# Second mamba block's input: from TensorE turns to block transfers and VectorE turns

## The chip, the core and the metric

One core of one Trainium2 chip runs the whole program. The metric is device time in microseconds (us), lower is better. The kernel before took 1117.68 us (median of 3 runs, 1117.55 to 1117.88).

## What is computed

The reference is a stack of four layers over 2 sequences of 1024 tokens with 512 features. Each layer adds its output to its input and normalises the sum. Only the first layer, a mamba-2 block, is touched here. Cut to what matters:

```python
zxbcdt = einsum('bld,di->bli', hidden_states, W_in)     # 512 -> 1024 gate | 1024 x | 16 B | 16 C | 16 dt
gate, xBC, dt = split(zxbcdt)
xBC = silu(conv4_causal(xBC) + conv_b)                  # 4 taps along the tokens, by channel
dt  = softplus(dt + dt_bias);  dA = exp(-exp(A_log) * dt)
h_t = h_{t-1} * dA_t + (dt_t * x_t) (x) B_t             # 16 heads of 64 by 16 states
y_t = h_t . C_t + D_skip * x_t
out = rmsnorm(y * silu(gate)) * norm_w @ W_out
x   = layernorm(x + out)
```

The later layers (a ternary projection, a gated recurrence, a dequantised SwiGLU) are the same in both kernels.

## The kernel before

The 2048 tokens are worked on in four blocks of 512 tokens (`TB`), called 0 to 3 here. For the first projection TensorE needs the block's input with features on the partitions: a tile `xT` of 128 partitions by 4 groups (k) by 512 tokens, of which two buffers exist. It comes in two ways.

- **Blocks 0 and 1**: `transposed` (lines 227 to 254) takes the token tiles `X[b]`, which are loaded anyway, and turns them on TensorE: 16 transposes of 128x128 into four PSUM banks (`pt`, line 237), each bank then copied to `xT`. For block 1 ScalarE makes all four copies (line 251, `by_act`).
- **Blocks 2 and 3**: `load_blocks` (line 260) reads the same input again from HBM in four transfers of 256 KB, in pieces of 32 floats (128 bytes), so that 32x32 squares lie where they have to be; `turn_blocks` (line 271) then turns the squares in place on VectorE, four instructions of 128x512.

`head(b, st)` (line 378) makes `xT`, then the small projection `pbc` (line 393: eight matmuls in order of k, two for each k, which give B, C and dt), and what follows from it. For block 1 it stops at its first `yield`, after `pbc` has been copied out, its convolution started and its rows sent by a transfer on SP's queue (line 410).

The opening of block 0 is written out by hand in `opening` (line 624). It runs under a manual schedule for TensorE, VectorE and ScalarE: these three engines run their instructions in the order of the text. It interleaves

- `inner(m)`: the projection `px` of x, eight times (line 372, four matmuls in two passes each), with the first tap of its convolution on ScalarE (line 355); the rest of a convolution is three VectorE taps (line 361) and a silu on ScalarE (line 365). The convolutions wait in the list `later`.
- `scans(h0)`: for four heads a broadcast `pl` on TensorE (line 574) and a scan on VectorE (line 578).
- `weigh(h0)`: `bdec` on VectorE (line 588) and four products on GpSimd (line 593).
- `next(g)`: a gate projection `pg` on TensorE (line 372) and its silu on ScalarE (line 747).
- `next(coming)`: `head(1)` up to its first `yield`.

The end of the opening has this order:

```python
scans(8); weigh(8)
later.append(inner(6)); next(g)
scans(12); weigh(12)
next(coming)                       # block 1: 16 transposes, 4 copies, pbc
later.pop(0)()                     # convolution 4
later.append(inner(7)); later.pop(0)()
for conv in later: next(g); conv() # convolutions 6 and 7
st["dtx"] = by_token(st, 0)        # pxt, line 674
```

`by_token` turns the result of the convolutions on TensorE (`pxt`), and the recurrence (`recur`, line 687) follows, with the rest of the gate projections between its steps. PSUM has eight banks, handed round among all these products.

On SP's queue before the opening stand, one after another, the input tokens of block 0, the weights `w_in`, the tokens `X[1]`, the weights `w_out` and the tokens `X[2]` (lines 84 to 134). `by_blocks(b, st)` (line 802) makes the tile `xT` and issues `load_blocks`; it is called for blocks 2 and 3.

Of the kernel before, what the change touches and what calls it, by code (L numbers as in the profile page):

```python
# [37 lines left out]
def model_kernel(ctx: ExitStack, tc: tile.TileContext, t: dict, out: bass.AP):  # L38
    nc = tc.nc
# [186 lines left out]
    def transposed(pool, b, X, tags=("xT",), split=False, bufs=1, by_act=False, behind=False, soon=False):  # L226


        pieces = [
            pool.tile([P, NK, TB], F32R if split else F32, tag=tag, name=f"{tag}{b}", bufs=bufs)  # L230
            for tag in tags
        ]
        xT = pieces[0]
        for k in range(NK):
            pt = bank("pt")
            for j in range(NJ):
                nc.tensor.transpose(  # L237
                    pt[:, j * P : (j + 1) * P], X[b][:, j, k * P : (k + 1) * P], ident
                )
            if split:  # L240
                copied = nc.scalar.copy(xT[:, k, :], pt)
                if behind:
                    tc.keep_in_program_order(copied)
                nc.vector.tensor_tensor(
                    pieces[1][:, k, :], pt, xT[:, k, :].bitcast(F32), ALU.subtract
                )
            elif soon:
                with tc.high_priority():
                    nc.scalar.copy(xT[:, k, :], pt)
            elif k % 2 or by_act:  # L250
                nc.scalar.copy(xT[:, k, :], pt)
            else:
                nc.vector.tensor_copy(xT[:, k, :], pt)
        return pieces
# [6 lines left out]
    def load_blocks(dst, rows, pinned=False):  # L261

        blocks = rows.rearrange("(n t) (k a c) -> a t k n c", t=32, k=NK, c=32)
        for a in range(4):
            load = nc.sync.dma_start(
                dst[32 * a : 32 * a + 32].rearrange("t k (n c) -> t k n c", c=32), blocks[a]
            )
            if pinned:
                tc.keep_in_program_order(load)

    def turn_blocks(dst, src=None, pinned=False):
        for k in range(NK):
            turned = nc.vector.transpose(dst[:, k, :], (src or dst)[:, k, :])
            if pinned:
                tc.keep_in_program_order(turned)
# [102 lines left out]
    def head(b, st):  # L378

        if b >= 3:  # L380
            X.append(tokens())
            nc.sync.dma_start(X[b], xin[b])
        if b > 1:
            xT = st["xT"]
            turn_blocks(xT, pinned=True)
        else:
            xT = st["xT"] = transposed(mp, b, X, bufs=2, by_act=b > 0)[0]

        pm = bank("pbc")
        half = TB // 2  # L390
        for k in range(NK):
            for i in range(2):
                nc.tensor.matmul(
                    pm[i * 64 : i * 64 + NR, :half], w_bc[:, k, :],
                    xT[:, k, i * half : (i + 1) * half], start=(k == 0), stop=(k == NK - 1),
                )
        rows = mp.tile([P, 3 + TB], F32, tag="xpad", name="rpad", bufs=3)
        for i in range(2):
            nc.scalar.copy(
                rows[:NR, 3 + i * half : 3 + (i + 1) * half], pm[i * 64 : i * 64 + NR, :half]  # L400
            )
        BC = st["BC"] = mp.tile([NBC, TB], F32, tag="BC", name="BC")

        mix = started(rows[:, 3:], NBC, b, NX, cwr, cbr, BC, rows)
        tk = sp.tile([P, 2, NJ, NH], F32, tag="tk", name="tk")
        dt, bt = st["dt"], st["bt"] = tk[:, 0], tk[:, 1]
        if b:

            turn = mp.tile([P, P], F32, tag="a2", name="turn")
            nc.sync.dma_start(  # L410
                turn[:HJ], rows[32:NR, 3:].rearrange("h (j t) -> h j t", t=P)
            )
        if b < 2:
            yield
        if b:

            mix(b == 1)
            nc.sync.dma_start(turn[HJ:], BC[:NS].rearrange("n (j t) -> n j t", t=P))
            nc.sync.dma_start(crow[b], BC[NS:])
            st["CT"] = mp.tile([P, TB], F32, tag="rows", name="CT", bufs=2)  # L420
            nc.sync.dma_start(st["CT"], crow[b].unsqueeze(0).to_broadcast([8, NS, TB]))
            yield
            yield from by_rows(b, turn, tk)
            return

        z = sp.tile([P, NJ, NH], F32, tag="z", name="z", bufs=1)
        a = sp.tile([P, NJ, NH], F32, tag="a", name="a", bufs=1)
        pdt = bank("pdt")
        for j in range(NJ):
            nc.tensor.transpose(  # L430
                pdt[:, j * NH : (j + 1) * NH], rows[32:NR, 3 + j * P : 3 + (j + 1) * P],
                ident[32:NR, 32:NR],
            )
        nc.vector.tensor_tensor(
            z, pdt[:, : NJ * NH].rearrange("p (j h) -> p j h", h=NH),
            dtb.unsqueeze(1).to_broadcast([P, NJ, NH]), ALU.add,
        )
        softplus(dt.rearrange("p j h -> p (j h)"), z.rearrange("p j h -> p (j h)"), NJ * NH)
        nc.vector.tensor_tensor(a, dt, rootA.unsqueeze(1).to_broadcast([P, NJ, NH]), ALU.mult)
        nc.vector.scalar_tensor_tensor(  # L440
            a, a, 1.0e18, rootN.unsqueeze(1).to_broadcast([P, NJ, NH]), ALU.min, ALU.mult
        )
        nc.vector.tensor_tensor(a, a, endless.unsqueeze(1).to_broadcast([P, NJ, NH]), ALU.min)
        for lo in (0, 32):
            nc.vector.tensor_scalar(a2[:, :, lo : lo + NH], a, LOG_FLOOR, None, ALU.max)
        yield
        pa = bank("pa")
        for j in range(NJ):
            nc.tensor.transpose(pa[:NR, j * P : (j + 1) * P], a2[:, j, :], ident)
        dA, cum = tmp("dA")[:NR], tmp("cum")[:NR]  # L450
        nc.scalar.activation(dA, pa[:NR, :], AF.Exp)

        r = st["r"] = mp.tile([NR, TB], F32R, tag="rows", name="rows", bufs=2)
        nc.scalar.activation(r, pa[:NR, :], AF.Exp)
        yield
        nc.vector.tensor_tensor(r[32:NR], dA[32:NR], r[32:NR].bitcast(F32), ALU.subtract)
        nc.vector.memset(r.bitcast(F32).rearrange("r (j t) -> r j t", t=P)[:, :, 0:1], 0.0)
        mix()
        yield
        for j in range(NJ):  # L460
            w = slice(j * P, (j + 1) * P)
            nc.vector.tensor_tensor_scan(
                cum[:, w], dA[:, w], zeros[:NR].to_broadcast([NR, P]), 1.0, ALU.mult, ALU.add
            )
        rc = st["rc"] = mp.tile([NR, TB], F32R, tag="rows", name="rows", bufs=2)
        nc.scalar.copy(rc, cum)
        yield
        nc.vector.tensor_tensor(rc[32:NR], cum[32:NR], rc[32:NR].bitcast(F32), ALU.subtract)
        yield
# [151 lines left out]
        st["dtx"] = by_token(st, 0)  # L621
        yield

    def opening(st, own, g, coming):


        inner, crows, grams, spans, scans, weigh = parts(0, st)
        first = inner(0)
        later = [inner(1)]
        next(own)  # L630
        first()
        next(own)
        later.append(inner(2))
        scans(0)
        later.append(inner(3))
        next(own)
        crows()
        later.pop(0)()
        next(own)
        later.append(inner(4))  # L640
        grams()
        spans()
        later.append(inner(5))
        weigh(0)
        later.pop(0)()
        scans(4)
        weigh(4)
        next(g)
        later.pop(0)()
        scans(8)  # L650
        weigh(8)
        later.append(inner(6))
        next(g)
        scans(12)
        weigh(12)
        next(coming)
        later.pop(0)()
        later.append(inner(7))
        later.pop(0)()
        for conv in later:  # L660
            next(g)
            conv()
        st["dtx"] = by_token(st, 0)
# [138 lines left out]
    def by_blocks(b, st):  # L802

        st["xT"] = mp.tile([P, NK, TB], F32, tag="xT", name=f"xT{b}", bufs=2)
        load_blocks(st["xT"], xin_rows[b])

    H, before, st = None, None, {}
    own, coming = head(0, st), {}
# [1 line left out]
    with tc.manual_schedule(  # L810
        engines={mybir.EngineType.PE, mybir.EngineType.DVE, mybir.EngineType.Activation}
    ):
        next(own)
        exponents(alog, endless, rootA, rootN)
        next(own)
        cwx, cbx, normw, dskip = columns_of_layer()
        opening(st, own, g, ahead)
    for b in range(NBLK):
        if b:
            g, coming = gates(b, st), {}  # L820
# [624 lines left out]
```

## Time and profile before

| | us |
|---|---|
| median of 3 runs | 1117.68 |
| the profiled execution | 1116.89 |
| its span, first to last instruction | 1115.1 |
| TensorE busy (PE) | 1099.4 |
| VectorE busy (DVE) | 701.4 |
| ScalarE busy (ACT) | 451.4 |
| GpSimd busy (POOL) | 366.8 |

The profile is of one execution, which took 0.79 us less than the median. Times in it count from the start of the span. In the timeline a row gives the start, the time from the first start to the last end of the merged instructions, the engine, the line, what is written from what, and in brackets the idle time before it with what ended it. PE is the matmul row of TensorE, PEld its weight loads. A float32 matmul is two passes, and so two rows ("x16" are eight matmuls).

### The profile page before, as it was taken

To read this page: it belongs to the slowest core of one execution; us is meant where nothing else is said; L and a number is where in the kernel's file an instruction comes from. 1 tells how busy PE (TensorE), PEld (TensorE's weight loads), DVE (VectorE), ACT (ScalarE), POOL (GpSimd) and SP (SyncE) were. 2 spreads that over 40 slices of the span, in tenths; PEclk is the share of its full clock that TensorE was granted. 3 is DMA by queue.
4 is the path that set the end of the run, shared out by engine and by line. 5 is a ranking of instruction groups with operands and counts; after the bars stand their busy time and mean duration, and the time that the engine had idled before them with its cause. 6 is when DMAs were issued, how large, how long until landed. Compare 5 with 4: busy or idle time off the path is not lost.

```text
span 1115.1 us, 12073 instructions
## 1 busy us (share of the span) xinstructions
PE 1099.4 (99%) x4450; PEld 663.3 (59%) x4450; DVE 701.4 (63%) x1267; ACT 451.4 (40%) x690; POOL 366.8 (33%) x347
## 2 busy tenths in 40 slices
PE   8999999999999999999999999999999999999996
PEld 5455445445544555745444444447888888888885
DVE  5989797797869676875727437184238866325224
ACT  3334624463454233556653372553223224224223
POOL 1547471565348240254433231236511001001000
PEclk9999999999999999999999999999999999999999
DMA  8005200911210137245650001304544002100001
GB/s 323 21 9 126 91 1 17 253 30 39 105 81 0 39 135 215 57 94 123 113 113 37 1 1 49 27 0 143 189 94 76 1 1 63 14 1 30 8 1 41
DMA packets 122059, 77.04 MB, mean 69 GB/s; under 512 B 94512, under 2 KB 95312, under 8 KB 120456
## 3 DMA queue, kind: packets, MB, share of 16 engines
q1 hardware_dynamic: 120792, 75.77, 25.7%
q8 instruction: 37, 0.61, 0.2%
q10 hardware_dynamic: 976, 0.39, 0.1%
q14 instruction: 30, 0.25, 0.1%
q0 software_dynamic: 224, 0.02, 0.0%
HBM read 59.95 MB, written 16.02 MB: 68 GB/s over the span
## 4 chain that ended last, share of the span: by engine, by line
PE 80%; DVE 11%; ACT 4%; issue 2%; POOL 2%; DMA 1%; SPq 0%; DVEq 0%; ACTq 0%; POOLq 0%
PE pgu L1039 20%; PE p L1069 16%; PE po L1270 10%; PE pg L372 9%; PE px L372 7%; PE po L770 6%; DVE acc L298 3%; PE po L1159 2%; PE py L705 2%; DVE L L578 2%; PE po L987 2%; PE pxt L674 1%; PE pt L237 1%; POOL x L1165 1%; PE py L697 1%
## 5 line engine op out<-in xcount | busy, mean ns | idle before, releaser
L1050 DVE SCALAR_TENSOR_TENSOR h<-pgu,L_ffn_up_scale,sg 128x512 f32<-128x512 f32 x63 | 47.1, 748 | 126.4 <-PE pgu L1039 122.6
L372 PE MATMUL px<-xT,w_in 128*128 128x512 f32 x256 | 114.6, 597 | 0.0
L593 POOL TENSOR_TENSOR L<-L,gm 128x512 f32<-128x512 f32 x64 | 93.5, 1490 | 63.7 <-DVE bdec L588 34.7
L372 PE MATMUL pg<-xT,w_in 128*128 128x512 f32 x256 | 113.5, 594 | 0.0
L770 PE MATMUL po<-w_out,xc 128*128 128x512 f32 x256 | 112.5, 593 | 0.7 <-DVE L L578 0.7
L1069 PE MATMUL p<-cv,w 128*128 128x512 f32 x256 | 110.8, 592 | 0.0
L1039 PE MATMUL pgu<-wF__4239,wg 128*128 128x512 f32 x256 | 101.7, 397 | 0.0
L1039 PE MATMUL pgu<-lo__4240,wg 128*128 128x512 f32 x256 | 100.8, 394 | 0.0
L1039 PE MATMUL pgu<-lo__4240,wu 128*128 128x512 f32 x256 | 100.7, 393 | 0.0
L1039 PE MATMUL pgu<-wF__4239,wu 128*128 128x512 f32 x256 | 100.7, 393 | 0.0
L1270 PE MATMUL po<-wd,hh 128*128 128x512 f32 x252 | 98.3, 396 | 0.3 <-POOL wg L930 0.3
L1270 PE MATMUL po<-wd,hl 128*128 128x512 f32 x252 | 98.3, 396 | 0.2 <-DVE hl L1054 0.2
L1049 ACT ACTIVATE sg<-pgu,L_ffn_gate_scale 128x512 f32<-128x512 f32 x63 | 43.4, 689 | 127.6 <-PE pgu L1039 127.6
L770 PEld LDWEIGHTS po<-w_out,xc 128*128 128x128 f32 x256 | 48.4, 190 | 61.8 <-issue 56.7
L1053 ACT CAST hh<-h 128x512 fp32r<-128x512 f32 x63 | 39.1, 621 | 112.5 <-DVE h L1050 112.3
L1069 PEld LDWEIGHTS p<-cv,w 128*128 128x128 f32 x256 | 48.6, 190 | 60.4 <-issue 58.8
L1069 PE MATMUL p<-xT,w 128*128 128x512 f32 x192 | 82.9, 592 | 0.0
L372 PEld LDWEIGHTS px<-xT,w_in 128*128 128x128 f32 x256 | 47.5, 190 | 57.5 <-issue 55.5
L298 DVE SCALAR_TENSOR_TENSOR acc<-xpad,cols,acc 128x512 f32<-128x512 f32 x72 | 68.5, 953 | 20.0 <-ACT acc L342 15.2
L372 PEld LDWEIGHTS pg<-xT,w_in 128*128 128x128 f32 x256 | 47.3, 190 | 54.2 <-issue 53.1
L1386 POOL TENSOR_TENSOR x<-x,r 128x512 f32<-128x512 f32 x12 | 15.2, 1295 | 195.0 <-DVE r L1385 195.0
L578 DVE TENSOR_TENSOR_SCAN L<-pl,id 128x512 f32<-128x512 f32 x64 | 75.0, 1205 | 4.7 <-ACT pl L572 3.7
(292 smaller groups left out, 1921.9 us busy)
## 6 DMA issues: line engine op xcount, KB each, us to landing
L<-decays SPq DMA_DIRECT2D x12, 1024.0 KB, 8.0
x_mid<-x SPq DMA_DIRECT2D x4, 1024.0 KB, 4.3
x<-x_mid SPq DMA_DIRECT2D x4, 1024.0 KB, 7.5
st<-in_L_ffn_gate_w_dram SPq DMA_DIRECT2D x8, 512.0 KB, 6.4
st<-in_L_ffn_up_w_dram SPq DMA_DIRECT2D x8, 512.0 KB, 4.4
st<-in_L_ffn_down_w_dram SPq DMA_DIRECT2D x8, 512.0 KB, 3.8
x_rec<-x SPq DMA_DIRECT2D x4, 1024.0 KB, 4.3
x<-_attn_hidden_states_dram SPq DMA_DIRECT2D x3, 1024.0 KB, 16.8
```

What stands on the lines that cost most here:

```text
L298: tap = nc.vector.scalar_tensor_tensor(acc, xpad[:, k : k + TB], w[:, k : k + 1], acc, ALU.mult, ALU.add)
L372: nc.tensor.matmul(pm[:n, :], w_in[:, k, lo : lo + n], xT[:, k, :], start=(k == 0), stop=(k == NK - 1),)
L578: nc.vector.tensor_tensor_scan(L[:, h, :], pl, id4.rearrange("p j t -> p (j t)"), 0.0, ALU.mult, ALU.add)
L593: nc.gpsimd.tensor_tensor(L[:, h, :], L[:, h, :], st["gm"], ALU.mult)
L705: nc.tensor.matmul(pys[i][hh * HD : (hh + 1) * HD, q, :], dtx[q][:, 2 * i + hh, :], L[:, h, s], start=(first and q == 0), stop=(q == 1), s ...
L770: nc.tensor.matmul(po, xc[:, m, j * P : (j + 1) * P], w_out[:, m, :], start=(m == 0), stop=(m == NX - 1),)
L1039: nc.tensor.matmul(pm, w[g][:, k, cols], x[:, k, :], start=(k == 0 and x is pieces[0]), stop=(k == NK - 1 and x is pieces[-1]),)
L1049: nc.scalar.activation(sg, pgu[0], AF.Silu, scale=gs[:, m : m + 1])
L1050: nc.vector.scalar_tensor_tensor(h, pgu[1], us[:, m : m + 1], sg, ALU.mult, ALU.mult)
L1053: nc.scalar.copy(halves[0], h)
L1069: nc.tensor.matmul(pm, w1[i][:, k, m * P : (m + 1) * P], rhs[:, k, :], start=(k == 0), stop=(k == NK - 1),)
L1270: nc.tensor.matmul(po[j], x[:, j * P : (j + 1) * P], wd[m // GK][:, m % GK, :], start=(m == 0 and x is h[0]), stop=(m == NF - 1 and x is h ...
```

## The change

Block 1 no longer uses `transposed`. Its `xT` is allocated and its four transfers are issued by `by_blocks(1)` just before the opening, kept in program order on SP's queue. Four VectorE turns, one for each k, are written into the opening: one after `scans(4)`, one after `scans(8)`, two after `scans(12)`, each ahead of the `weigh` that follows. `head(1)` starts with `pbc`. The tokens `X[1]` are loaded as before.

```diff
@@ head @@
-        if b > 1:
+        if b:
             xT = st["xT"]
-            turn_blocks(xT, pinned=True)
+            if b > 1:
+                turn_blocks(xT, pinned=True)
         else:
-            xT = st["xT"] = transposed(mp, b, X, bufs=2, by_act=b > 0)[0]
+            xT = st["xT"] = transposed(mp, b, X, bufs=2)[0]
@@ opening @@
-    def opening(st, own, g, coming):
+    def opening(st, own, g, coming, second):
...
         scans(4)
+        nc.vector.transpose(second[:, 0, :], second[:, 0, :])
         weigh(4)
         next(g)
         later.pop(0)()
         scans(8)
+        nc.vector.transpose(second[:, 1, :], second[:, 1, :])
         weigh(8)
         later.append(inner(6))
         next(g)
         scans(12)
+        nc.vector.transpose(second[:, 2, :], second[:, 2, :])
+        nc.vector.transpose(second[:, 3, :], second[:, 3, :])
         weigh(12)
         next(coming)
@@ by_blocks and its calls @@
-        load_blocks(st["xT"], xin_rows[b])
+        load_blocks(st["xT"], xin_rows[b], pinned=b == 1)
...
-        opening(st, own, g, ahead)
+        by_blocks(1, coming)
+        opening(st, own, g, ahead, coming["xT"])
```

## The prediction

> **What bounds the kernel now.** I read the busy table and the chain of the page first, then the timeline of each engine from 36 to 100 us, where everything that the change touches lies, and last the transfers.
>
> ```profile
> PE 1099.4 (99%) x4450; PEld 663.3 (59%) x4450; DVE 701.4 (63%) x1267; ACT 451.4 (40%) x690; POOL 366.8 (33%) x347
> ...
> PE 80%; DVE 11%; ACT 4%; issue 2%; POOL 2%; DMA 1%; SPq 0%; DVEq 0%; ACTq 0%; POOLq 0%
> ```
>
> TensorE is busy for 99% of the span and is 80% of the chain that ended last. So a microsecond of TensorE work removed is worth a microsecond, provided that TensorE then finds something to do; and a wait put before TensorE costs its whole length. TensorE around the transposes of block 1 (`pt`):
>
> ```profile
> 51.56 1.19 PE L574 MATMUL pl<-rows,pick 48*128 48x512 f32 x4
> 52.68 1.34 PE L237 MATMUL pt<-ident,x 128*128 128x128 f32 x8
> 54.48 1.09 PE L237 MATMUL pt<-ident,x 128*128 128x128 f32 x8 [0.46 <-DVE L L578]
> 55.59 1.93 PE L393 MATMUL pbc<-xT,w_bc 128*48 128x256 f32 x16
> 57.46 3.70 PE L372 MATMUL px<-xT,w_in 128*128 128x512 f32 x8
> 61.00 7.03 PE L372 MATMUL pg<-xT,w_in 128*128 128x512 f32 x16
> ```
>
> There is one small idle in them, 0.46 us inside the transposes themselves. VectorE in the same stretch:
>
> ```profile
> 39.15 4.56 DVE L578 TENSOR_TENSOR_SCAN L<-pl,id 128x512 f32<-128x512 f32 x4 [0.23 <-PE pl L574]
> 43.75 0.42 DVE L588 TENSOR_TENSOR bdec<-L,tk 128x256 f32<-128x256 f32 x1
> 44.09 2.31 DVE L361 SCALAR_TENSOR_TENSOR acc<-px,cols,acc 128x509 f32<-128x509 f32 x3
> 46.32 4.55 DVE L578 TENSOR_TENSOR_SCAN L<-pl,id 128x512 f32<-128x512 f32 x4
> 50.91 0.42 DVE L588 TENSOR_TENSOR bdec<-L,tk 128x256 f32<-128x256 f32 x1
> 52.09 4.57 DVE L578 TENSOR_TENSOR_SCAN L<-pl,id 128x512 f32<-128x512 f32 x4 [0.76 <-PE pl L574]
> 56.69 0.42 DVE L588 TENSOR_TENSOR bdec<-L,tk 128x256 f32<-128x256 f32 x1
> 57.03 8.98 DVE L361 SCALAR_TENSOR_TENSOR acc<-px,cols,acc 128x509 f32<-128x509 f32 x12
> ```
>
> VectorE is nearly full too: it idles for 0.76 us before the last scans and then not until 66.01. So both engines are loaded here, and the change takes work from one and gives it to the other, at a place where the first must wait for the second. That is the question to be worked out.
>
> **What goes.** The 16 transposes (two rows of x8) and the idle between them: from 52.68 to 55.59, **2.91 us of TensorE**. Four copies on ScalarE go as well (2.34 us in all between 53.38 and 56.24); ScalarE has gaps of over a microsecond on both sides of them, so I count them at nothing. Nobody else waits for either.
>
> **What comes on SP's queue.** Four transfers, behind `X[2]`, whose issue ends at 18.34, and ahead of the line 410 transfer, whose issue comes at 58.35 when ScalarE has made its rows; nothing stands between. The load at the start uses every DMA engine until about 29.5:
>
> ```profile
> 18.00:29.00 11.00, 11.00 (x30) 4.63 (x28) 9.96 (x15) 5.72 (x10) 0.00 (x0) 1.00 1.04 387
> 31.00:43.00 12.00, 12.00 (x39) 5.75 (x37) 10.20 (x17) 3.83 (x9) 4.96 (x4) 1.00 0.00 1
> 106.00:112.00 6.00, 6.00 (x21) 2.97 (x20) 4.51 (x4) 2.00 (x5) 5.76 (x5) 1.00 1.41 155
> ```
>
> The last two columns of these stretches are the DMA share and GB/s. The third stretch is the same kind of load for block 2, in pieces of 128 bytes: 155 GB/s. Block 1's 1.05 MB would take 6.8 us at that rate; if none of it moves before 29.5, it has landed at about 36.3, in a stretch in which the DMA engines do nothing today. The first turn wants it at 43.6. That is 7 us in hand, so I cost the transfers at nothing: the empty DMA engines hide them. Without that cover every microsecond of lateness would hold VectorE at the first turn, with the convolutions and scans queued behind it, and so TensorE. `w_out` and `X[2]`, which could be slowed, are not read before 90.
>
> **What comes on VectorE.** Four turns. The trace has the same instruction for block 2:
>
> ```profile
> 166.36 2.48 DVE L273 STREAM_TRANSPOSE xT<-xT 128x512 f32<-128x512 f32 x4
> ```
>
> One takes 0.67 us (664 to 705 ns over block 2 and 3), so they follow each other by (2.48 - 0.67) / 3 = 0.60 us. The scans take 1.205 us each by the page and follow each other by (4.57 - 1.205) / 3 = 1.12. `bdec` must wait for the last scan to be written, so today it starts 4.60 after the first scan; a turn needs nothing from the scans and can start 4.49 after it. With these steps, VectorE runs so:
>
> - Turn 0 starts at 39.15 + 4.49 = 43.64, `bdec` at 44.24 instead of 43.75: 0.49 late. Convolution 3 and scans 8 to 11 follow, from 46.81.
> - Turn 1 at 51.30, `bdec` at 51.90 (0.99 late), after which VectorE is free at 52.24. Today it stood idle until 52.09, waiting for `pl`; that idle pays for most of the first two turns. Scans 12 to 15 begin at 52.24, only **0.15 late**.
> - Turn 2 at 56.73, ending at 57.40; turn 3 at 57.33, ending at **58.00**. The last `bdec` starts at 57.93, 1.24 late.
>
> **What TensorE now waits for.** With the transposes gone it comes to `pbc` at 52.68. The two instruction lists, set side by side, differ on TensorE only in the 16 transposes and in what the matmuls from `pbc` on wait for: the second, third and fourth k of `pbc` wait for VectorE, each for its turn. The bank that `pbc` takes is free when the second gate's silu has read it, at 52.27. The first two k take half of 1.93, to 53.64. The third k can start when turn 2 is written, and TensorE follows VectorE by 0.04 us (the second scan ended at 54.44, `pt` went on at 54.48): 57.44. **TensorE stands for 3.80 us.** The third k takes 0.48, the fourth starts at 58.04 after another 0.12, and `px` of m = 7 starts at 58.52. Today it starts at 57.46. So the sum is 3.80 + 0.12 of waiting, 2.91 saved, and 0.05 for the two hand-overs: **1.06 us late**. The order of the text is what costs: the last two turns stand behind scans 12 to 15, and TensorE has nothing between `pl` and `pbc` but the transposes that are taken out.
>
> **What is late next.** TensorE runs `px` and two `pg` without a gap, then `pxt`, whose last part waits for ScalarE's last silu, and that stands behind the last gate's silu:
>
> ```profile
> 68.06 0.60 ACT L747 ACTIVATE g<-pg 128x512 f32<-128x512 f32 x1 [2.31 <-PE pg L372]
> 68.56 0.62 ACT L365 ACTIVATE xc<-acc 128x512 f32<-128x512 f32 x1
> ```
>
> Convolution 7 ends at 66.01 today, 2.55 before this silu begins. It will end 1.24 later and the silu 1.06 later, so 2.37 remain and VectorE does not set this end. GpSimd's last products end at 62.17 today and are 1.24 later; they are read from 69.49 on. After that the lists of all engines are alike, and every start depends on TensorE's or VectorE's earlier work, not on a clock time; TensorE has only 0.95 us of waiting for VectorE between 70 and 100 (92.79 and 94.00), and that chain begins with `pxt` and moves with it. I take none of it as absorbed; were all of it absorbed, 0.1 would be left.
>
> Bounds: with turns of 0.71 us following by 0.65, as the slowest rows have it, and with 0.1 for each hand-over, the four turns give about 0.3 more, 1.4 in all. The least is 0.1 by absorption. I take 1.1, nearest to the rows. The profiled execution took 1116.89, which becomes 1118.0; it stood 0.79 under the median of the runs, so for the median 1117.68 + 1.1 = **1118.8**.
>
> **A stand of 3.8 us and the clock.** No row of this kernel has TensorE wait for longer than 1.4 us before its last matmul, so the trace does not show what such a stand does to its clock. It shows one longer stand, at the end (last columns: granted clock, DMA share, GB/s):
>
> ```profile
> 1106.50:1111.00 4.50, 0.00 (x0) 0.00 (x0) 3.33 (x10) 1.61 (x5) 1.54 (x2) 1.00 0.49 179
> 1111.20:1115.00 3.80, 0.00 (x0) 0.00 (x0) 0.00 (x0) 0.00 (x0) 0.00 (x0) 0.50 0.23 82
> ```
>
> The last matmul ends at 1106.46; the clock was still full 4.5 us later and half after that. By this row a stand of 3.8 is just short enough. The Trainium skill, "TensorE: Matmul & The Clock Gate", section "The HAM clock gate", speaks against the change: the array falls to half its clock after one idle window of about 3.4 us, and the windows run freely. By that rule an estimate is that a stand of 3.8 holds a whole window in (3.8 - 3.4) / 3.4, some 12%, of executions, and then about 3.4 us of work at half the clock would cost 1.7 us more; the trace's own end, 4.5 us or more, does not contradict it.
>
> **Rivals.**
>
> *The clock falls in the stand (slower).* Place: `px` of m = 7, just after `pbc`. Price: at least what the start of the trace shows, where the first 24 rows of 128x128 (`early`, from 1.43) took 4.73 us and 24 at the pace of the transposes (1.09 for 8) would take 3.27, so 1.46 more; at most all of `px` at half speed, 3.54 more. It decides if it falls in most executions. For it: the stand is near the one after which the clock fell. Against: full at 4.5 us. The sum is 1.06 + 1.46 to 3.54: 1120.2 to 1122.3, say 1121.2.
>
> *The transfers are late (slower).* They would have to land after 44.8 to move the time past 1120; for it: small pieces at 155 GB/s, behind 2 MB of `w_out`. Against: 7 us in hand. Say 1120.5.
>
> *The 2.91 us are kept (faster).* If `pbc` did not stand there waiting, because the turns were done before TensorE came to it, `px` would start at 54.55. Turn 3 would have to end by 54.1, before the scans it stands behind. Against: the order of the list, which has both turns behind those scans, and no other TensorE work between. 1117.68 - 2.91 = 1114.8.
>
> *Absorbed.* The 0.95 us of waiting swallow most: 1117.8.
>
> **How the numbers follow.** The forecast, 1118.4 to 1119.4, gets 0.68; absorbed 0.09; the clock 0.13; late transfers 0.05; kept 0.05. A measurement of this kernel can tell about 0.2%, 2.2 us, from no change. The forecast and the absorbed case lie within it, with a little of the late transfers: 0.78. Above it lie the clock and the rest: 0.17. Below, 0.05. The range goes from the absorbed case, 1117.8, to the lower part of the clock's, 1120.8, and leaves out about 0.05 below and 0.1 above.
>
> **What the profile will show.** Right: no `pt` rows after 10 us; `pbc` in two parts with 3.5 to 4.2 us of idle between, ended by VectorE's turn; scans 12 at 52.1 to 52.5; `px` 7 at 58.4 to 59; `pxt` at 68.9 to 69.4; turns of 0.67; the block load landed by 38. Wrong: `px` 7 before 57.4 (something fills the gap), passes of `px` 7 over 0.8 us (the clock), a turn 0 that waits for a DMA, or a later wait of TensorE that has shrunk by the same microsecond.

## The result and the profile after

The changed kernel took **1120.36 us** (median of 8 runs, 1119.49 to 1121.06), the kernel before 1117.04 beside it (8 runs, 1116.85 to 1117.88): a ratio of 1.0028, 95% interval 1.0018 to 1.0039. It is 3.3 us slower. The forecast of the likeliest case was 1.1 slower; the time lies in the part of the range that belonged to the rival "the clock falls in the stand" (1120.2 to 1122.3). The profiled execution took 1120.36, its span is 1118.6.

| us | forecast | measured |
|---|---|---|
| block 1's transfers landed | 36.3 | between 37 and 38 |
| turn 0 starts | 43.64 | 43.70 |
| scans 12 to 15 start | 52.24 | 52.22 |
| `pbc` third k starts, after a stand of TensorE of | 57.44, 3.80 | 57.43, 3.61 |
| the last `bdec` starts | 57.93 | 57.90 |
| `px` of m = 7 starts | 58.52 | 59.31 |
| `pg` after it starts (before 61.00; forecast 1.06 later) | 62.06 | 64.38 |

First the busy line of the page, which says little: TensorE has 16 matmuls less (4434 rows for 4450) and yet the same busy time, and its share has gone down.

```profile
PE 1099.2 (98%) x4434; PEld 661.9 (59%) x4434; DVE 703.4 (63%) x1271; ACT 449.0 (40%) x686; POOL 366.7 (33%) x347
```

VectorE's timeline in the changed kernel (start, time, engine, line, what is written from what):

```profile
52.22 4.55 DVE L579 TENSOR_TENSOR_SCAN L<-pl,id 128x512 f32<-128x512 f32 x4
56.70 0.68 DVE L658 STREAM_TRANSPOSE xT<-xT 128x512 f32<-128x512 f32 x1
57.30 0.67 DVE L659 STREAM_TRANSPOSE xT<-xT 128x512 f32<-128x512 f32 x1
57.90 0.38 DVE L589 TENSOR_TENSOR bdec<-L,tk 128x256 f32<-128x256 f32 x1
```

Each of these starts within 0.03 of its forecast: the turns take 0.67 to 0.68, follow each other by 0.60, and stand behind the scans. TensorE's timeline:

```profile
52.75 1.07 PE L394 MATMUL pbc<-xT,w_bc 128*48 128x256 f32 x8
57.43 1.95 PE L394 MATMUL pbc<-xT,w_bc 128*48 128x256 f32 x8 [3.61 <-DVE xT L658]
59.31 5.23 PE L372 MATMUL px<-xT,w_in 128*128 128x512 f32 x8
64.38 7.03 PE L372 MATMUL pg<-xT,w_in 128*128 128x512 f32 x16
```

The stand is where it was forecast, for the reason forecast (the bracket names the turn of the third k, line 658). But the two halves of `pbc` are the same eight rows, and the second takes 1.95 for 1.07; `px`, which took 3.70 before, takes 5.23. The stretches of the trace tell why (columns: the busy time of PE, PEld, DVE, ACT and POOL with their instructions, then granted clock, DMA share, GB/s):

```profile
52.20:55.60 3.40, 1.62 (x11) 0.61 (x9) 3.40 (x5) 0.13 (x1) 3.22 (x3) 1.00 0.00 0
55.60:59.00 3.40, 1.57 (x8) 0.61 (x8) 3.36 (x7) 0.00 (x0) 2.36 (x3) 0.50 0.00 0
59.00:62.40 3.40, 3.40 (x6) 1.52 (x5) 3.29 (x5) 2.07 (x4) 3.40 (x4) 0.50 0.05 10
62.40:66.00 3.60, 3.60 (x9) 1.52 (x8) 3.04 (x5) 1.36 (x3) 1.04 (x2) 1.00 0.02 5
```

The granted clock is half from 55.60 to 62.42. It fell 1.78 after TensorE's last row had ended (53.82), in the middle of the stand. From `pg` on the shift against the kernel before stays 3.38 (`pxt` at 71.24 for 67.86), and the span is 3.5 longer: nothing is absorbed later. The mean clock was 0.995 or 0.996 in all 8 runs, and 0.998 in the profile of before, so this is no accident of one execution (a window of 6.83 us at half clock takes 0.003 off the mean).

### The profile page after: what moved, and what is told of

The parts are those of the page before. It is cut to its first block, busy times and chain, and to the rows that moved or that the text cites. A ratio compares the mean times of both kernels' runs of the same rounds, so it can differ in the third digit from the quotient of the medians.

```text
span 1118.6 us, 12047 instructions
## 1 busy us (share of the span) xinstructions
PE 1099.2 (98%) x4434; PEld 661.9 (59%) x4434; DVE 703.4 (63%) x1271; ACT 449.0 (40%) x686; POOL 366.7 (33%) x347
## 4 chain that ended last, share of the span: by engine, by line
PE 81%; DVE 11%; ACT 4%; issue 1%; POOL 1%; DMA 1%; SPq 0%; DVEq 0%; ACTq 0%; POOLq 0%
PE pgu L1045 20%; PE p L1075 18%; PE po L1276 10%; PE pg L372 8%; PE px L372 6%; PE po L775 6%; DVE L L579 3%; DVE acc L298 3%; PE po L993 3%; PE po L1165 2%; PE py L710 2%; PE pxt L679 1%; PE pt L237 1%; POOL x L1171 1%; PE py L702 1%
```

## The experiments

My theory: of the 3.3 us, 1.1 is the stand itself, as forecast, and 2.2 the clock that falls in it. The rivals: the clock is a bystander, and the rest beyond 1.1 comes from what the turns and transfers do elsewhere, on VectorE with all that queues behind the turns, or later in the kernel. The first two kernels shorten the stand of TensorE without moving any turn; the other four move the turns or TensorE's work, to see whether the 2.91 us can be had at all. The first four ran on one chip with a kernel before of 1117.12 (33 runs, 1116.95 to 1117.33), the last two on another with 1117.33 (21 runs, 1116.79 to 1117.90). Each experiment has 11 runs.

### 1. TensorE kept busy in the stand (1118.21 us)

In `head`, inside the loop over k of `pbc`; nobody reads the bank:

```diff
+            if b == 1 and k == 2:
+                fill = bank("fill")
+                for _ in range(13):
+                    nc.tensor.matmul(fill[:, :P], ident, ident, start=True, stop=True)
```

> The changed kernel, with 13 matmuls of the identity by itself put between the second and the third k of block 1's pbc, so that TensorE works through the 3.6 us for which it stood; they write a bank that nobody reads. Theory A (the stand costs 1.06 net, and the rest of the 3.3 us is the clock at half behind it): pbc and px of m = 7 at full pace again (0.97 and 3.7 us), granted clock 1.00 throughout 52 to 66, time about 1.1 over the kernel before, 1118.1. Rival B (the slow passes come from reading what VectorE has just written, or from PSUM, not from the stand): px stays at 5.2 us, time stays 3.3 over, 1120.4. Rival C (filling makes no difference because VectorE sets the end): 1120.4 as well, with px at 3.7 and pxt late by a convolution.

Measured: 1118.21 (1118.05 to 1118.45), 1.0010 of before (1.0001 to 1.0019). TensorE's timeline, and one stretch with the clock in the third column from the right:

```profile
53.67 3.17 PE L396 MATMUL fill<-ident 128*128 128x128 f32 x26
57.36 1.23 PE L398 MATMUL pbc<-xT,w_bc 128*48 128x256 f32 x8 [0.52 <-DVE xT L662]
58.52 3.70 PE L372 MATMUL px<-xT,w_in 128*128 128x512 f32 x8
```

```profile
52.00:66.00 14.00, 13.48 (x64) 7.42 (x63) 13.75 (x19) 4.11 (x9) 10.06 (x9) 1.00 0.02 4
```

`pbc` goes on at the same time as without the filling (57.36 for 57.43), the clock stays full, `px` takes 3.70 again, and it starts at 58.52: to the hundredth what the prediction had. More work on TensorE makes the kernel faster. Against the kernel before of the same chip the filled kernel is 1.09 slower, and the changed kernel 3.32 slower: 1.1 is the turns' lateness, **2.2 the clock**. The filling leaves every turn, transfer and queue of the changed kernel where it was, so whatever theory puts the 2.2 on one of those falls.

### 2. Half of the filling (1119.57 us)

The same with `range(6)`.

> As the run with 13, but with 6 matmuls: TensorE works until about 55.2 and stands for 2.1 us only. Theory A, if a stand must be about as long as the 3.6 us to bring the clock down: clock 1.00, 1118.1. Theory A, if part of a window of idle is enough (the clock fell 1.8 us after the stand began in the changed kernel): the clock falls in some executions, times spread from 1118.1 to 1120.4. Rival B: 1120.4.

Measured: 1119.57 (1118.08 to 1120.47), 1.0017 (1.0008 to 1.0026). The median hides two groups: four executions at 1118.08 to 1118.11, with a mean clock of 0.997 or 0.998, and seven at 1118.71 to 1120.47, six of them with 0.996 (the one at 1118.71 has 0.998). The profile is of one of the seven:

```profile
57.45 1.23 PE L398 MATMUL pbc<-xT,w_bc 128*48 128x256 f32 x8 [2.08 <-DVE xT L662]
58.61 5.40 PE L372 MATMUL px<-xT,w_in 128*128 128x512 f32 x8
```

```profile
55.30:58.60 3.30, 1.22 (x9) 0.34 (x8) 3.30 (x6) 0.00 (x0) 2.27 (x3) 1.00 0.00 0
58.70:62.00 3.30, 3.30 (x4) 1.39 (x5) 3.16 (x6) 2.18 (x4) 3.30 (x3) 0.50 0.08 15
```

A stand of 2.08 is enough to bring the clock down, in about half of the executions, and it falls *after* the stand: `pbc` runs at full clock (1.23) and `px` not. The four that are spared take the time of the first experiment. So the length of a stand does not settle alone what it costs.

### 3. The turns earlier, TensorE's order kept (1117.52 us)

```diff
         scans(4)
         nc.vector.transpose(second[:, 0, :], second[:, 0, :])
+        nc.vector.transpose(second[:, 1, :], second[:, 1, :])
...
         scans(8)
-        nc.vector.transpose(second[:, 1, :], second[:, 1, :])
+        nc.vector.transpose(second[:, 2, :], second[:, 2, :])
+        nc.vector.transpose(second[:, 3, :], second[:, 3, :])
...
         scans(12)
-        nc.vector.transpose(second[:, 2, :], second[:, 2, :])
-        nc.vector.transpose(second[:, 3, :], second[:, 3, :])
```

> The changed kernel with its turns moved up: two after scans 4 to 7, two after scans 8 to 11, none after scans 12 to 15. By the working of the prediction (the place of the last two turns makes the stand): no stand before pbc, px of m = 7 at about 54.7, VectorE's last convolution ends 1.4 us later than before, at 67.4, and its silu frees pxt at 68.0 instead of 69.2: time 1.2 under the kernel before, 1115.8, clock full. Rival (VectorE had no room, any turn on it costs its length): 1.0 or more over before, 1118 to 1119.

Measured: 1117.52 (1116.20 to 1117.76), 1.0000 (0.9991 to 1.0009). Again two groups: five executions at 1116.20 to 1116.32 (mean clock 0.997), six at 1117.52 to 1117.76 (0.996). TensorE in one of the five:

```profile
54.67 3.70 PE L372 MATMUL px<-xT,w_in 128*128 128x512 f32 x8
...
66.18 0.33 PE L679 MATMUL pxt<-ident,xc 128*128 128x128 f32 x1 [0.29 <-ACT xc L365]
68.47 0.33 PE L679 MATMUL pxt<-ident,xc 128*128 128x128 f32 x1 [1.96 <-ACT xc L365]
```

`px` starts at 54.67 for 57.46: nearly all of the 2.91 us has arrived there. But the last parts of `pxt` now wait 0.29 and 1.96 for the silus, and those for VectorE's convolutions, which the four turns and a `bdec` of 0.79 instead of 0.42 push from 57.03 to 58.71. After this wait 0.77 is left (`py` at 68.72 for 69.49), and that is what the five executions gain (0.9 under the kernel before). The expected 1115.8 was missed by 0.4 there. The other six lose 1.39 more, with a lower mean clock; that a stand of about 2 brings the clock down in some executions only is what experiment 2 showed, but no profile here is of one of the six.

### 4. `px` of m = 7 moved before `pbc`, whole (1116.90 us)

```diff
         weigh(12)
+        later.append(inner(7))
         next(coming)
         later.pop(0)()
-        later.append(inner(7))
         later.pop(0)()
```

> The changed kernel with the projection px of m = 7 moved ahead of block 1's pbc, the turns left where the change put them: TensorE has 3.6 us of real work in the stand. Theory A: px from 52.7 to 56.3, pbc from 56.3 with under 0.5 us of waiting, clock full, pxt freed by the last silu at about 68.0: 1.2 under the kernel before, 1115.8. Rival B (slow passes from something other than the stand): px or pbc slow, over 1117. Rival (the gain cannot be had since VectorE is the bound): 1117 to 1118.5.

Measured: 1116.90 (1116.76 to 1117.10), 0.9998 (0.9989 to 1.0007): the expected gain of 1.3 is missing. It is there at 68 (`py` at 68.04 for 69.49) and is lost at 95. The rows of ScalarE and VectorE there:

```profile
93.39 1.28 ACT L489 ACT_TABLE_LOAD   x1 [8.57 <-DVE work L488]
...
95.02 0.42 DVE L490 TENSOR_TENSOR_SCAN work<-work,zeros 64x128 f32<-64x128 f32 x1 [1.72 <-ACT work L489]
```

and one row of the kernel before:

```profile
95.14 0.48 DVE L489 TENSOR_TENSOR_SCAN work<-work,zeros 64x128 f32<-64x128 f32 x1 [0.38 <-ACT work L488]
```

Before, ScalarE loads the table for its next exp at 86.29, while it has nothing to do. Here the load waits for VectorE's `work` at 93.39, and the 1.28 it takes stands on the path. I had moved `inner(7)` with its ScalarE tap, which changes ScalarE's order and the order in which the small rotating buffers are handed out. My reading is that the exp then has to wait for two engines, and that one of the two waits is put on the load; that this is the reason is argued and not shown, and the next kernel, which leaves ScalarE's order alone, speaks for it. On TensorE the loss appears at 126.34, where it waits for VectorE's scans, which follow from the row at 95.02:

```profile
126.34 7.13 PE L775 MATMUL po<-w_out,xc 128*128 128x512 f32 x16 [1.52 <-DVE L L579]
```

The kernel before waits 0.24 there and goes on at 126.52: of the 1.45 gained at 68, 0.18 is left.

### 5. Only the matmuls of `px` moved (1115.65 us)

```diff
-        def inner(m):
-            px = in_proj(xT, DI + m * P, P, "px")
+        def inner(m, px=None):
+            px = px or in_proj(xT, DI + m * P, P, "px")
...
+        px7 = in_proj(st["xT"], DI + 7 * P, P, "px")
         next(coming)
         later.pop(0)()
-        later.append(inner(7))
+        later.append(inner(7, px7))
```

> As the run with px of m = 7 ahead of pbc, but only its matmuls go ahead; its first tap on ScalarE stays behind pbc's copies, so that the rotating buffers of the small tiles are handed out in the order of the changed kernel. In the run before, the recurrence began 1.45 us earlier than in the kernel before, and 1.28 of that was lost at 95 us, where VectorE waited 1.72 us (0.38 in the kernel before) for ScalarE, whose table load for the exponential stood behind VectorE's result at 93.39 instead of being done at 86.29. Theory A (the gain was lost in that table load alone): the load is done in ScalarE's idle time again, and the whole 1.45 stays: 1115.7. Rival (VectorE's own chain of work takes the gain back): 1116.9 again.

Measured: **1115.65** (1115.47 to 1116.39), 0.9986 (0.9977 to 0.9995), faster than both kernels. TensorE:

```profile
52.63 3.70 PE L372 MATMUL px<-xT,w_in 128*128 128x512 f32 x8
56.26 2.29 PE L394 MATMUL pbc<-xT,w_bc 128*48 128x256 f32 x16
...
67.85 0.33 PE L680 MATMUL pxt<-ident,xc 128*128 128x128 f32 x1 [1.47 <-ACT xc L365]
```

The turns are as late as in the changed kernel. The 3.70 of `px`, which needs none of them, now fill the stand; `pbc` loses 0.36 (2.29 for 1.93) and nothing more. The table load is early again (84.90), the scan's wait 0.38. `pxt` stands for 1.47, and the mean clock is 0.997 or 0.998 in all 11 runs. `py` starts at 68.11, 1.38 earlier than before.

### 6. The turns sooner still, and the transfers first (1115.29 us)

Block 1's four transfers are issued ahead of `X[1]`, `w_out` and `X[2]`; two turns go into the 1.13 us in which VectorE stands idle near 33, two after scans 8 to 11:

```diff
+    second_xT = load_second()          # before the load of X[1]
...
         next(own)
+        nc.vector.transpose(second[:, 0, :], second[:, 0, :])
+        nc.vector.transpose(second[:, 1, :], second[:, 1, :])
         later.append(inner(4))
...
         scans(8)
+        nc.vector.transpose(second[:, 2, :], second[:, 2, :])
+        nc.vector.transpose(second[:, 3, :], second[:, 3, :])
```

> The changed kernel with block 1's four transfers put ahead of those of X[1], w_out and X[2] on SP's queue, two turns put where VectorE stood idle for 1.13 us at 33.3, and two after scans 8 to 11, where it stood for 0.76. By the prediction's working (only turns beyond VectorE's idle time cost): VectorE's last convolution ends about 0.4 later than in the kernel before, at 66.4, TensorE has no stand before pbc, pxt is freed at about 67.2 and py starts near 67.4 instead of 69.5: 2.1 under the kernel before, 1115.0, if TensorE's stand before pxt (1.2 us) leaves the clock alone. If the transfers are not in by 33.3, or slow those of w_in down: over 1116. If a turn costs its length wherever it stands: 1116 or more.

Measured: **1115.29** (1115.04 to 1115.84), 0.9983 (0.9974 to 0.9992), the best of all. VectorE has two of its turns at 33.39 and 34.02; TensorE:

```profile
54.59 3.70 PE L382 MATMUL px<-xT,w_in 128*128 128x512 f32 x8
...
67.42 0.33 PE L689 MATMUL pxt<-ident,xc 128*128 128x128 f32 x1 [1.50 <-ACT xc L375]
```

The convolutions start at 57.66, 0.63 late instead of the 1.68 of experiment 3, so the stand before `pxt` is 1.50 instead of 1.96, and the clock stays up in all 11 runs (0.997 to 0.999). `py` starts at 67.68, 1.81 earlier than before. In the profiled execution 0.60 of that is given back at 125.30, where TensorE waits 0.84 for block 1's scans (0.24 before). They are late because two small VectorE instructions at 92.06 and 92.91 took 0.81 and 0.63 instead of 0.33 and 0.52. The profiled execution of experiment 2 shows the same (0.82 and 0.63, then a wait of 0.83), the other profiles do not, so this does not come from the place of the turns; why it happens stays open.

The times of this chip lie in two groups some 0.5 to 0.6 apart, here (1115.04 to 1115.29 and 1115.68 to 1115.84) as in the kernel before (1116.79 to 1117.05 and 1117.33 to 1117.90). Lower group against lower group the gain is 1.9, which fits the 1.81 of `py`, and that of experiment 5 is 1.4, which fits its 1.38; the medians give 2.0 and 1.7.

## Why the prediction was right and wrong

- *"2.91 us of TensorE"* go: right. In experiment 3, where nothing stands before `pbc`, `px` starts 2.79 earlier.
- *Transfers at nothing*: right. They landed 1 to 1.7 later than I had it, and still some 6 before the first turn; no turn waits for a DMA.
- *Four turns of 0.67 by steps of 0.60, scans 0.15 late, the last two turns behind scans 12 to 15*: right within 0.06 in the three rows of the table that show them.
- *"TensorE stands for 3.80 us"*: 3.61, since the first half of `pbc` drains until 53.82, not 53.64. Where it goes on, and so what it costs, was right: 57.43.
- *"1.06 us late"*: right as the price of the order. The filled kernel has `px` at 58.52 as forecast and takes 1.09 more.
- *Absorbed*: nothing was. The shift is 3.38 at 64 and at 71, and still 3.36 at 130.
- **The step that failed: "By this row a stand of 3.8 is just short enough."** I read the end of the trace, where the clock was still full 4.5 us after the last matmul, as the length of stand that the clock bears. It bears less than half of that: it fell 1.78 after TensorE's last row in the profiled execution, and by the mean clock it fell in all 8. What that row really showed was where a window ends. The recorded changes of the clock lie on a grid: in the changed kernel full from 4.40, half from 55.60, 15 steps of 3.413; in experiment 2 7.48 and 58.68, 15 steps; in the kernel before 5.20 and 1111.12, 324 steps. At the end of the trace before, the window that closed at 1107.7 held 1.25 of idle time and left the clock up; the next one closed at 1111.12. The 4.5 was a phase, and no limit.
- *The rule of the Trainium skill* ("TensorE: Matmul & The Clock Gate", "The HAM clock gate": half clock after one idle window of about 3.4 us), which I took to mean a window idle from end to end: the step of the grid agrees, the need for a whole idle window does not. In the changed kernel the window from 52.18 to 55.60 had TensorE at work until 53.82, and the clock fell at its end. The measurement decides; the estimate of 12% of executions made from the rule was far too low, since it was 8 of 8.
- *The price, 1.46 to 3.54*: right. 2.2 by the medians, and 2.32 by `pg` (64.38 for 62.06).
- *The chance of 0.13* was therefore the error, not the mechanism: the forecast's own terms gave 1.1, and the rival was added to it. The forecast, 1118.4 to 1119.4, was missed by 1.0; that the measured 1120.36 lies inside the range (up to 1120.8) is luck, since the range only took in the lower part of a rival held unlikely.
- *The signs*: `pbc` in two parts with 3.61 between, scans 12 at 52.22, turns of 0.67 to 0.69 and the load before 38 came as listed. `px` came at 59.31, after the 58.4 to 59 listed, `pxt` at 71.24 and not at 68.9 to 69.4, and with passes of `px` of up to 1.22 the sign of the clock was there.
- *Kept, 1114.8*: its condition (turns done before TensorE comes to `pbc`) was met in experiments 3 and 6, and the full 2.91 was not kept even so. I had worked out that convolution 7 has 2.37 in hand against the last gate's silu, and did not use it there: a TensorE that runs 2.8 earlier and a VectorE that runs 0.6 to 1.7 later use it up, and `pxt` stands for 1.5 to 2.

## What to carry to other kernels

Price a new stand of TensorE twice, once for its length and once for the clock that falls in it, and take the second as likely from about 2 us on (half of the executions here at 1.96 and 2.08, all at 3.61, none at 1.5), even where the first is nearly paid for by work removed. When work is handed from the bound engine to another, ask what the bound engine does until it comes back: putting a product that needs none of it into the gap (experiment 5), or the handed work into the other engine's idle time well before (experiment 6), turned 3.3 us lost into 1.7 and 2.0 gained by the medians. Move the matmuls alone, and leave the other engines' order as it is: the same move with a ScalarE instruction in tow gained 0.2 instead of 1.7 (experiments 4 and 5).

## What the hardware showed that was not expected

How often the clock fell, by the longest stand of TensorE in the profiled execution behind 50 us and the mean clock of the runs (one window of 3.41 us at half clock takes 0.0015 off the mean; 0.996 and less counts as down):

| stand, us | kernel | clock down |
|---|---|---|
| 3.61 | changed | 8 of 8 |
| 2.08 | experiment 2 | 6 of 11 |
| 1.96, with 0.29 just before | experiment 3 | 6 of 11 |
| 1.40 to 1.52 | experiments 4, 5, 6 | 0 of 33 |

One reading fits all four rows: the clock falls at the end of a window of 3.41 us that holds more than some 1.6 to 1.8 us of idle time, wherever the windows happen to lie, and rises at the end of a busy one. The windows of the profiled executions, laid out from the recorded changes of the clock, bound it:

| window | kernel | idle time in it, us | clock at its end |
|---|---|---|---|
| 64.42 to 67.84 | experiment 3 | 1.61 | stays full |
| 52.18 to 55.60 | changed | 1.78 | falls |
| 55.27 to 58.68 | experiment 2 | 2.08 | falls |
| 1106.24 to 1109.65 | experiment 1, its end | 2.09 | falls |
| 59.01 to 62.42 | changed | none | rises |

By an estimate from these rows, with 1.65 as the limit: a stand of 3.61 always leaves at least 1.8 in one of two windows; one of 2.08 does so at (3.41 - 2.08 + 2 x 0.43) / 3.41 = 64% of the phases, one of 1.96 at 61%, one of 1.5 never. The two bounds, 1.61 and 1.78, are measured; that the phase decides within one kernel is argued, since only one execution of each was profiled. In the changed kernel the clock stayed down for two windows (6.83 us), the second of which began with 1.83 of the same stand; in experiment 2 for one (3.41), in which `px` took 1.70 longer (5.40 for 3.70).
